# VectorE's side work moved between v and scan, experts' sums over two ticks, gate ranks by broadcast comparison, group norm sums on ScalarE

## The chip, the cores and the metric

The kernel runs on one core of a Trainium2 chip. The metric is device time in microseconds of one execution. Before the change it is 3911.06 us, the median of three runs (3910.29 to 3911.66). All data are fp32.

The names of the profile: PE is TensorE's matmul and PEld its weight load; DVE is VectorE, ACT is ScalarE, POOL is GpSimd, SP is SyncE, which here issues the DMAs.

## What is computed

Four images of 384 channels and 32 x 32 positions pass through two layers:

```python
# layer 0: group norm, then a selective scan in four directions over the image
x = x + _L0_conv_ref(_gn(x), ...)
#   dt = softplus(dts + bias); for each direction k and each position:
#     h = h * exp(dt * A) + (dt * u) * B        (16 states a channel)
#     y = sum over states of h * C
#   directions are summed, y + D * u, layer norm over channels, gelu
# layer 1: attention and a mixture of 4 experts, of which the best 2 count
t = _to_tokens(x)
t = t + _L1_attn_ref(_ln_t(t), Wq, Wk, Wv)      # causal, one head of 384
t = t + _L1_ffn_ref(_ln_t(t), gate_w, gate_b, w1, b1, w2, b2)
#   probs = softmax(scores); keep the top 2 of 4 and renormalise
#   out = sum over experts of masked * (gelu(x w1 + b1) w2 + b2)
```

## The kernel before

The program is laid out by hand in *ticks*. A tick is one unit of the scan: 32 channels by 4 states on the 128 partitions, 1024 positions along each. There are 4 images x 3 blocks of 128 channels x 4 directions x 4 groups of states x 4 groups of channels = 768 units, 192 an image. The loop over ticks writes instructions into the queues of the engines in a fixed order; nothing reorders them afterwards. In tick t it does this:

- `decay(t + 2)`: ScalarE computes exp(dt * A) (`da`, L505).
- `due`: functions that were put off to this tick. They stand ahead of v, that is after the scan of the tick before.
- `front(t)`: VectorE multiplies dt*u (`du4`, from SBUF) by B (`bc`, from SBUF) into `v` in PSUM (L512).
- `back(t - 1)`: GpSimd multiplies the states of the unit before by C (`h<-h,bc`, L525, "the product"). Both inputs are in SBUF. `order` makes it wait for v of tick t, so that it runs beside the scan.
- `inner`: functions put off to the place between v and scan; then `unpark` resumes the generators that had yielded "inner".
- `middle(t)`: VectorE's scan (L518), which reads `da` from SBUF and `v` from PSUM.
- `row`: after every fourth unit TensorE sums the states over partitions with the matrix `sel` (L550, the "y row").
- `fetch`: loads for coming units; then one step of `preparation` (group norm, projections and softplus of the next image), and `go_on`, which advances the side work and the work that waits in turn.

A generator that yields "wait", n is resumed n ticks later from the last place of the tick, so its VectorE work stands after the scan. One that yields "inner" is resumed in the next tick between v and scan.

The work behind the scan of an image is: `finish` (layer norm, gelu L702, residual add L707), `attention` (layer norm with L601, L633 and L649, queries, values, scores, softmax with L780 and L782, `normalise` with L794 and L795), `gates` (L881 to L923: softmax of four scores and their ranks, by loops over the four experts), and `experts` (matmuls L1027 and L1052, sums L1061 and L1064). `behind` runs attention and experts of one image after those of the other. They are metered: a tick may issue as much matmul as `pace`, in units of about a microsecond, PACE_A in attention and PACE_E in the experts. Image b's experts therefore run beside the scan of image b+1, and those of the last image alone.

Further names: `groupnorm` (statistics L302 and L303 on VectorE), `project_dt` (softplus L387, then du = dt * u, L395, stored by SP for the loads of later ticks), `evict` (L570). `slots` and `banks` are pools of SBUF buffers and PSUM banks that the program hands out in ticks. The buffer `a0` holds the attention's input `axn`, and then the experts' sums, which `store` writes out.

Of the kernel before, what the change touches and what calls it, by code (L numbers as in the profile page):

```python
# [15 lines left out]
P = 128  # L16
# [24 lines left out]
BANKS = 4  # L41
SLOTS = 8
PACE_A = 4.4
PACE_E = 3.3


@with_exitstack
def hybrid_kernel(
# [46 lines left out]
    clock = [-100]  # L95
    due = {}
    inner = {}

    def defer(ticks, f, where=due):
        where.setdefault(clock[0] + ticks, []).append(f)  # L100
# [99 lines left out]
    a4 = const.tile([P, K * NG, NQ], F32, tag="a4", name="a4")  # L200

    sel = const.tile([P, DJ], F32, tag="sel", name="sel")
    dump = const.tile([P, 1], F32, tag="dump", name="dump")
    nc.scalar.activation(a_raw, a_raw, AF.Exp)
    nc.scalar.activation(dump, eps, AF.Sqrt)
# [91 lines left out]
    def groupnorm(b, u):  # L297
        st = sm.tile([P, M, NH, 6], F32, tag="gn_st", name=f"gn_st_{b}")
        mv = sm.tile([P, M, 2], F32, tag="gn_mv", name=f"gn_mv_{b}")
        for m in range(M):  # L300
            for h in range(NH):
                nc.vector.bn_stats(st[:, m, h, :], u[m][:, h * 512 : (h + 1) * 512])  # L302
            nc.vector.bn_aggr(mv[:, m, :], st[:, m].rearrange("p h s -> p (h s)"))  # L303
            if b == 0 and m == 0:
                pgb = group_weights()
            yield "wait", 1
        if b == 0:
            nc.vector.tensor_scalar_mul(gback, pgb[:NGRP, :C], float(C // NGRP))
        mean_c = sm.tile([P, M], F32, tag="gn_mc", name=f"gn_mc_{b}")
        nc.vector.tensor_copy(mean_c, mv[:, :, 0])  # L310
        yield "wait", 1
        mean = sm.tile([P, M], F32, tag="gn_mean", name=f"gn_mean_{b}")
        ps = yield from over_group(mean_c, f"mean_{b}")
        nc.vector.tensor_copy(mean, ps)
        banks.give(f"gn_mean_{b}")
        dev = sm.tile([P, M], F32, tag="gn_dev", name=f"gn_dev_{b}")
        nc.vector.tensor_sub(dev, mean_c, mean)
        nc.vector.tensor_mul(dev, dev, dev)
        nc.vector.tensor_add(dev, dev, mv[:, :, 1])
        yield "wait", 1  # L320
        rstd = sm.tile([P, M], F32, tag="gn_rstd", name=f"gn_rstd_{b}")
        ps = yield from over_group(dev, f"var_{b}")
        nc.scalar.activation(rstd, ps, AF.Sqrt, bias=eps)
        banks.give(f"gn_var_{b}")
        yield "wait", 1
        nc.vector.reciprocal(rstd, rstd)
        nc.vector.scalar_tensor_tensor(mean, mean, -1.0, rstd, ALU.mult, ALU.mult)
        for m in range(M):
            if b == 0 and m == 1:
                nc.vector.tensor_scalar(  # L330
                    u[m], u[m], rstd[:, m : m + 1], mean[:, m : m + 1], ALU.mult, ALU.add
                )
            else:
                nc.scalar.activation(
                    u[m], u[m], AF.Identity, bias=mean[:, m : m + 1], scale=rstd[:, m : m + 1]
                )
            nc.sync.dma_start(xn_d[b][:, m, :], u[m])
            yield "wait", 1
# [26 lines left out]
    def project_dt(b, pair, m, u, xd):  # L365

        ks = PAIRS[pair]
        while not slots.ready(3 + pair):
            yield "wait", 1
        v = u[m]  # L370
        if pair == 1:
            v = slots.now(f"ut_{b}_{m}", P, L)
            nc.scalar.copy(v.rearrange("p (w h) -> p w h", h=HW), columns(u[m]))
        dts = [slots.now(f"dt_{b}_{k}_{m}", P, L) for k in ks]
        for h in range(NH):
            while not banks.ready(2):
                yield "wait", 1
            pss = [banks.now(f"pdt_{b}_{k}_{m}_{h}") for k in ks]
            for i, k in enumerate(ks):
                r = slice(64 * pair + 32 * i, 64 * pair + 32 * i + R)  # L380
                nc.tensor.matmul(  # L381
                    pss[i], wdt[r, m * P : (m + 1) * P], xd[r, bass.ts(h, 512)],
                    start=True, stop=True,
                )
            yield "wait", 1
            for i, k in enumerate(ks):
                nc.scalar.activation(  # L387
                    dts[i][:, bass.ts(h, 512)], pss[i], AF.Softplus, bias=dtb[:, k, m : m + 1]
                )
                banks.give(f"pdt_{b}_{k}_{m}_{h}")  # L390
        yield "wait", 1
        for i, k in enumerate(ks):
            nc.sync.dma_start(dts_d[b, k][0, m * P : (m + 1) * P, :], dts[i])
            du = yield from slots.take(f"du_{b}_{k}_{m}", P, L)
            nc.vector.tensor_mul(du, dts[i], v)  # L395
            yield "wait", 1
            nc.sync.dma_start(dts_d[b, k][1, m * P : (m + 1) * P, :], du)
            slots.give(f"dt_{b}_{k}_{m}", f"du_{b}_{k}_{m}")
        if pair == 1:
            slots.give(f"ut_{b}_{m}")  # L400
# [179 lines left out]
    def layernorm(dst, src, name, lag):  # L580
# [48 lines left out]
            rs, var[:, : n * P].rearrange("p (h t) -> p h t", t=P), AF.Sqrt, bias=eps  # L629
        )  # L630
        banks.give(f"var_{name}")
        yield "wait", 1
        nc.vector.reciprocal(rs, rs)  # L633
        yield "wait", lag
        backs = []
# [56 lines left out]
    def finish(b):  # L692

        yb = ybs[b]
        yield from layernorm(yb, yb, f"l0_{b}", 0)
        xrs = []
        for m in range(M):
            xr = yield from slots.take(f"xr_{b}_{m}", P, L)
            nc.sync.dma_start(xr, x[b, m * P : (m + 1) * P, :])
            xrs.append(xr)  # L700
        for m in range(M):
            nc.scalar.activation(  # L702
                yb[:, m, :], yb[:, m, :], AF.Gelu, bias=lnb[:, m : m + 1], scale=lnw[:, m : m + 1]
            )

            def add(m=m, xr=xrs[m]):
                nc.vector.tensor_add(yb[:, m, :], xr, yb[:, m, :])  # L707
                slots.give(f"xr_{b}_{m}")
                if m == M - 1:
                    finished.add(b)  # L710

            defer(1 + m // 2, add)

    def attention(b, yb, fx0):
        xn = ap0.tile([P, M, L], F32, tag="a0", name=f"axn_{b}")
# [61 lines left out]
        def softmax(i, ss, pr):  # L777
# [5 lines left out]
            for n, (o, e, ps) in enumerate(ss):  # L783
# [2 lines left out]
                    accum_out=nb[:, 2 + n : 3 + n],  # L786
                )
                banks.give(f"ss_{b}_{i}_{o}")
            defer(1, lambda: normalise(i, nb, len(ss)))

        def normalise(i, nb, n):
            wd = (i + 1) * P
# [75 lines left out]
    def gates(b, h, xn):  # L868
# [7 lines left out]
                    start=(c == 0), stop=(c == M - 1),  # L876
                )
        yield "pe", 5.0
        yield "wait", 1
        sc = sm.tile([P, 4, E], F32, tag="sc", name=f"sc_{name}")  # L880
        nc.vector.tensor_tensor(  # L881
            sc, pg[:, : 4 * E].rearrange("p (q e) -> p q e", e=E),
# [9 lines left out]
        nc.vector.tensor_reduce(red, sc, AX.X, ALU.max)  # L892
        nc.vector.tensor_tensor(sc, sc, over(red), ALU.subtract)
        nc.scalar.activation(sc, sc, AF.Exp)
        yield "wait", 1
        nc.vector.tensor_reduce(red, sc, AX.X, ALU.add)
        nc.vector.reciprocal(red, red)
        nc.vector.tensor_tensor(sc, sc, over(red), ALU.mult)
        cnt = sm.tile([P, 4, E], F32, tag="cnt", name=f"cnt_{name}")
        cmp = sm.tile([P, 4, E], F32, tag="cmp", name=f"cmp_{name}")  # L900
        nc.vector.memset(cnt, 0.0)
        for d in range(E):

            other = sc[:, :, d : d + 1]
            if d > 0:
                nc.vector.tensor_tensor(
                    cmp[:, :, :d], other.to_broadcast([P, 4, d]), sc[:, :, :d], ALU.is_gt
                )
                nc.vector.tensor_add(cnt[:, :, :d], cnt[:, :, :d], cmp[:, :, :d])
            if d < E - 1:  # L910
                nc.vector.tensor_tensor(
                    cmp[:, :, d + 1 :], other.to_broadcast([P, 4, E - 1 - d]),
                    sc[:, :, d + 1 :], ALU.is_ge,
                )
                nc.vector.tensor_add(cnt[:, :, d + 1 :], cnt[:, :, d + 1 :], cmp[:, :, d + 1 :])
            if d % 2:
                yield "wait", 1
        mk = sm.tile([P, 4, E], F32, tag="mk", name=f"mk_{name}")
        nc.vector.scalar_tensor_tensor(mk, cnt, 1.5, sc, ALU.is_lt, ALU.mult)
        nc.vector.tensor_reduce(red, mk, AX.X, ALU.add)  # L920
        nc.vector.tensor_scalar_add(red, red, 1e-9)
        nc.vector.reciprocal(red, red)
        nc.vector.tensor_tensor(mk, mk, over(red), ALU.mult)  # L923
        yield "wait", 1
        pm = yield from banks.take(f"pm_{name}")
        nc.tensor.transpose(pm[: 4 * E, :P], mk.rearrange("p q e -> p (q e)"), ident)
        yield "pe", 0.3
# [25 lines left out]
    def experts(b, acc, xns):  # L953
# [43 lines left out]
        def store(h):  # L997
            o = h * 512
            nc.sync.dma_start(out[b, :, o : o + 512].rearrange("(m p) l -> p m l", p=P), acc)
            if h + 1 < NH:  # L1000
                defer(4, lambda: load(h + 1))

        load(0)
        for h, e in [(h, e) for h in range(NH) for e in range(E)]:
# [37 lines left out]
            for c, (m, fh) in enumerate(TWO):  # L1042
# [15 lines left out]
                if fh == 1:  # L1058

                    def out_(m=m, ps=pss[m], e=e, tw=tw, fy=fy):  # L1060
                        nc.vector.scalar_tensor_tensor(  # L1061
                            ps, ps, b2s[:, e, m : m + 1], tw, ALU.add, ALU.mult
                        )
                        nc.vector.tensor_add(acc[:, m, :], acc[:, m, :], ps)  # L1064
                        banks.give(fy)

                    defer(2, out_, inner)
            if e == E - 1:
# [1 line left out]
                defer(4, lambda h=h: store(h))  # L1070

    pace = [PACE_E]

    def behind(b):
        while b not in finished:
            yield "wait", 1
        pace[0] = PACE_A
        fx0 = one.tile([P, M, 512], F32, tag="fx0", name=f"fx0_{b}")
# [79 lines left out]
    while t < NU + 4 or waiting or side or due or inner or parked:  # L1158
# [5 lines left out]
        done = None  # L1164
        if t < NU:
            done = front(t)
        if 1 <= t <= NU:
            back(t - 1, done)
        for f in inner.pop(t, []):
            f()  # L1170
        unpark()
        if t < NU:
            middle(t)
        if t >= 2 and t - 2 < NU and (t - 2) % NJ == NJ - 1:
# [62 lines left out]
```

## Time and profile before

| | us |
|---|---|
| median of the runs | 3911.06 |
| the profiled execution | 3911.65 |
| its span, first to last instruction | 3909.9 |
| busy PE | 3382.8 (87%) |
| busy DVE | 3096.5 (79%) |
| busy ACT | 1887.9 (48%) |
| busy POOL | 1809.5 (46%) |
| first v / last v | 49.3 / 3233.7 |

The mean granted TensorE clock is 0.899 of full speed.

The page cuts the span into 40 slices of 97.7 us; a digit is the busy share of a slice in tenths. A group line reads: line, engine, operation, output<-inputs, shapes, count | busy us in all, mean ns of one | idle time of the engine just before them, and what ended most of it. A line of the table by stretches reads: from:to in us, length, then busy us and number of records of PE, PEld, DVE, ACT and POOL, then granted clock, DMA share and GB/s. An fp32 matmul leaves two records. A timeline line reads: start, duration, engine, line, what it does, count, and in brackets the idle time before it and what ended that.

Some groups that the change concerns, as VectorE's groups by line have them:

```profile
L1061 DVE SCALAR_TENSOR_TENSOR fy<-fy,b2s,tw 128x512 f32<-128x512 f32 x96 | 72.3, 754 | 424.1 <-PE fy L1052 424.1
...
L302 DVE BATCH_NORM_STATS2 gn_st<-x 128x6 f32<-128x512 f32 x24 | 15.1, 673 | 3.6 <-DMA x<-in_x 3.6
L707 DVE TENSOR_TENSOR yb<-xr,yb 128x1024 f32<-128x1024 f32 x12 | 14.5, 1234 | 2.6 <-ACT yb L702 2.6
...
L782 DVE TENSOR_TENSOR nb<-nb 128x1 f32<-128x1 f32 x16 | 9.9, 619 | 0.5
```

### The profile page before, as it was taken

What the parts mean: (1) busy time and instruction counts of PE and PEld (TensorE: products, weight loads), DVE (VectorE), ACT (ScalarE), POOL (GpSimd) and SP (SyncE); (2) the same over time, 40 slices, a digit from 0 to 9 for tenths busy, and PEclk for the clock granted to TensorE, in tenths of its full rate; (3) what the DMA queues carried; (4) which work ended last, traced back from release to release, by engine and by line L of the source; (5) the groups of instructions that cost most, each with busy time, mean ns of one, the idle gap of its engine ahead of it and who ended that gap; (6) DMA issues with size and microseconds to landing.
All of it is one profiled execution on the core that took longest, in us unless ns stands there. A gap on an engine that the chain in (4) does not pass through costs nothing.

```text
span 3909.9 us, 32087 instructions
## 1 busy us (share of the span) xinstructions
PE 3382.8 (87%) x10623; PEld 1389.4 (36%) x10623; DVE 3096.5 (79%) x2258; ACT 1887.9 (48%) x1996; POOL 1809.5 (46%) x776
## 2 busy tenths in 40 slices
PE   4554655659899999978999999799999998999999
PEld 1100100015433334435433343354334334644444
DVE  6999999998999999979999899989999993110000
ACT  5442543446656656546656545555455453322121
POOL 2665666654555556535555566455566661000000
PEclk7665666679899999989999999899999999999999
DMA  5554545453576667535666666426566651132321
GB/s 192 203 183 148 197 147 188 162 189 127 191 239 208 236 223 241 184 112 190 223 211 214 212 218 213 162 105 227 179 214 213 222 187 44 61 90 82 96 82 55
DMA packets 406087, 671.85 MB, mean 172 GB/s; under 512 B 33265, under 2 KB 280353, under 8 KB 405921
## 3 DMA queue, kind: packets, MB, share of 16 engines
q1 hardware_dynamic: 399712, 669.41, 50.5%
q8 instruction: 84, 1.38, 0.1%
q10 hardware_dynamic: 6208, 0.39, 0.1%
q14 instruction: 83, 0.67, 0.1%
HBM read 597.75 MB, written 71.96 MB: 171 GB/s over the span
## 4 chain that ended last, share of the span: by engine, by line
DVE 49%; PE 38%; issue 5%; ACT 4%; DMA 2%; POOL 1%; DVEq 1%; SPq 0%; POOLq 0%; ACTq 0%
DVE h L518 29%; DVE v L512 15%; PE ph L1027 13%; PE fy L1052 12%; PE y L550 3%; PE ss L766 2%; PE pq L737 2%; PE pv L748 2%; PE po L832 1%; ACT da L505 1%; DVE fy L1061 1%; ACT ht L1016 1%; PE pxd L350 1%; DMA du<-dts 1%; DVE du L395 1%
## 5 line engine op out<-in xcount | busy, mean ns | idle before, releaser
L525 POOL TENSOR_TENSOR h<-h,bc 128x1024 f32<-128x1024 f32 x768 | 1808.4, 2355 | 1430.0 <-DVE v L512 1278.1
L518 DVE TENSOR_TENSOR_SCAN h<-da,v 128x1024 f32<-128x1024 f32 x768 | 1755.5, 2286 | 86.1 <-DVE v L512 1.5
L505 ACT ACTIVATE da<-dt,a 128x1024 f32<-128x1024 f32 x768 | 878.0, 1147 | 1232.3 <-DVE h L518 1171.7
L1027 PE MATMUL ph<-fx,w 128*128 128x512 f32 x2304 | 1027.5, 602 | 9.4 <-ACT ht L1012 3.8
L1052 PE MATMUL fy<-ht,w 128*128 128x512 f32 x2304 | 1015.8, 598 | 2.4 <-ACT dt L387 0.9
L512 DVE TENSOR_TENSOR v<-du,bc 128x1024 f32<-128x1024 f32 x768 | 947.2, 1233 | 38.5 <-DMA du<-dts 16.4
L550 PE MATMUL y<-h,sel 128*32 128x512 f32 x3072 | 703.7, 713 | 309.5 <-POOL h L525 295.3
L1027 PEld LDWEIGHTS ph<-fx,w 128*128 128x128 f32 x2304 | 434.8, 192 | 588.9 <-issue 530.7
L1052 PEld LDWEIGHTS fy<-ht,w 128*128 128x128 f32 x2304 | 435.5, 191 | 570.5 <-issue 551.7
L1012 ACT ACTIVATE ht<-ph,b1s 128x512 f32<-128x512 f32 x384 | 257.6, 679 | 453.0 <-PE ph L1027 452.5
L550 PEld LDWEIGHTS y<-h,sel 128*32 128x32 f32 x3072 | 118.3, 118 | 831.7 <-POOL h L525 579.2
L1061 DVE SCALAR_TENSOR_TENSOR fy<-fy,b2s,tw 128x512 f32<-128x512 f32 x96 | 72.3, 754 | 424.1 <-PE fy L1052 424.1
L1016 ACT ACTIVATE ht<-ht 128x3072 f32<-128x3072 f32 x64 | 176.9, 2764 | 0.8
L505 ACT ACT_TABLE_LOAD x110 | 141.1, 1283 | 14.4 <-DMA dt<-dts 12.5
L766 PE MATMUL ss<-axn,qt 128*128 128x512 f32 (+3 forms) x288 | 105.3, 512 | 7.4 <-ACT yb L844 5.8
L832 PE MATMUL po<-pt,vt 128*128 128x256 f32 x480 | 103.6, 363 | 6.7 <-ACT pt L728 6.7
L832 PEld LDWEIGHTS po<-pt,vt 128*128 128x128 f32 x480 | 91.9, 193 | 21.7 <-ACT pt L728 9.2
L780 DVE TENSOR_REDUCE nb<-ss 128x1 f32<-128x512 f32 (+3 forms) x48 | 26.2, 554 | 82.8 <-PE ss L771 64.6
L381 PE MATMUL pdt<-xd,wdt 12*128 12x512 f32 x184 | 61.5, 690 | 34.4 <-ACT xd L354 26.5
L766 PEld LDWEIGHTS ss<-axn,qt 128*128 128x128 f32 x288 | 52.3, 199 | 53.3 <-issue 36.5
L1064 DVE TENSOR_TENSOR fx<-fx,fy 128x512 f32<-128x512 f32 x96 | 65.9, 687 | 3.3
L1016 ACT ACT_TABLE_LOAD x50 | 64.2, 1283 | 0.9
(183 smaller groups left out, 1406.5 us busy)
## 6 DMA issues: line engine op xcount, KB each, us to landing
bc<-rows SPq DMA_DIRECT2D x384, 512.0 KB, 4.7
w<-in_w SPq DMA_DIRECT2D x384, 384.0 KB, 6.0
dt<-dts SPq DMA_DIRECT2D x192, 512.0 KB, 4.0
du<-dts SPq DMA_DIRECT2D x192, 512.0 KB, 6.1
dts<-dt SPq DMA_DIRECT2D x48, 512.0 KB, 4.9
dts<-du SPq DMA_DIRECT2D x48, 512.0 KB, 4.6
fx<-t2d SPq DMA_DIRECT2D x12, 768.0 KB, 6.0
tw<-mkd SPq DMA_DIRECT2D x32, 256.0 KB, 5.7
```

What stands on the lines that cost most here:

```text
L505: nc.scalar.activation(u["da"], spread["dt4", n], AF.Exp, scale=a4[:, g, u["q"] : u["q"] + 1])
L512: return nc.vector.tensor_tensor(u["v"], spread["du4", n], spread["bc", n][:, 0, :], ALU.mult)
L518: nc.vector.tensor_tensor_scan(u["h"][:, ::step], u["da"][:, ::step], u["v"][:, ::step], 0.0, op0=ALU.mult, op1=ALU.add,)
L525: product = nc.gpsimd.tensor_tensor(h, h, spread["bc", n][:, 1, :], ALU.mult)
L550: nc.tensor.matmul(y, sel, h, start=first, stop=last, tile_position=(0, jj * DJ))
L766: nc.tensor.matmul(ps[:, : e - o], qt[:, c, i * P : (i + 1) * P], xn[:, c, o:e], start=(c == 0), stop=(c == M - 1 and e <= i * P),)
L832: nc.tensor.matmul(pv[:, o:], vt[:, j, m * P : (m + 1) * P], pts[step][j // 4][:, j % 4, o:], start=False, stop=(j == nj - 1),)
L1012: nc.scalar.activation(ht[:, f, :], ps, AF.Identity, bias=bias)
L1016: nc.scalar.activation(ht, ht, AF.Gelu)
L1027: nc.tensor.matmul(ps, tiles[n][:, c, (f % 2) * P : (f % 2 + 1) * P], xns[h][:, c, :], start=(c == 0), stop=(c == M - 1),)
L1052: nc.tensor.matmul(pss[m], tiles[n][:, f, :], hts[fh][:, f, :], start=(fh == 0 and f == 0), stop=(fh == 1 and f == FH - 1),)
L1061: nc.vector.scalar_tensor_tensor(ps, ps, b2s[:, e, m : m + 1], tw, ALU.add, ALU.mult)
```

## The change

- Side work of VectorE that stood after the scan now stands between v and scan: du (L395), the residual add (L707), the reciprocals of the layer norms (L633), the softmax's normalise, and all of the gates.
- `back` is issued after `inner` and `unpark`. The product waits for the last of v, du and the residual add of its tick (the list `both`); other work between v and scan does not hold it back.
- The experts' two operations an output, the weighted bias and the sum, go into two successive ticks.
- The ranks of the gates are computed by two comparisons of all pairs, a mask `lower`, a maximum and a reduction, instead of loops over experts.
- For images 1 to 3 the group norm's sums come from ScalarE's accumulators (six passes over an image, three of Identity and three of Square) instead of VectorE's statistics.
- Attention of an image waits until the store of the image before has been issued (`stored`).
- PACE_E is 3.4 instead of 3.3.

```diff
-PACE_E = 3.3
+PACE_E = 3.4
...
+    both = []
...
+    lower = const.tile([P, E, E], F32, tag="lower", name="lower")
+    nc.vector.memset(lower, 0.0)
+    for e in range(1, E):
+        nc.vector.memset(lower[:, e, :e], 1.0)
...
-        for m in range(M):
+        mean_c = sm.tile([P, M], F32, tag="gn_mc", name=f"gn_mc_{b}")
+        if b > 0:
+            var_c = sm.tile([P, M], F32, tag="gn_vc", name=f"gn_vc_{b}")
+            sq = yield from slots.take(f"gn_sq_{b}", P, L)
+            for m in range(M):
+                nc.scalar.activation(
+                    sq, u[m], AF.Identity, scale=-1.0 / L, accum_out=mean_c[:, m : m + 1]
+                )
+                yield "wait", 1
+            for m in range(M):
+                nc.scalar.activation(
+                    sq, u[m], AF.Square, bias=mean_c[:, m : m + 1], accum_out=var_c[:, m : m + 1]
+                )
+                yield "wait", 1
+            slots.give(f"gn_sq_{b}")
+            yield "inner", 0
+            nc.vector.tensor_scalar_mul(mean_c, mean_c, -1.0)
+            nc.vector.tensor_scalar_mul(var_c, var_c, 1.0 / L)
+        for m in range(M) if b == 0 else ():
...
-        yield "wait", 1
         for i, k in enumerate(ks):
             nc.sync.dma_start(dts_d[b, k][0, m * P : (m + 1) * P, :], dts[i])
             du = yield from slots.take(f"du_{b}_{k}_{m}", P, L)
-            nc.vector.tensor_mul(du, dts[i], v)
+            yield "inner", 0
+            both[:] = [nc.vector.tensor_mul(du, dts[i], v)]
...
-        yield "wait", 1
+        yield "inner", 0
         nc.vector.reciprocal(rs, rs)
...
-                nc.vector.tensor_add(yb[:, m, :], xr, yb[:, m, :])
+                both[:] = [nc.vector.tensor_add(yb[:, m, :], xr, yb[:, m, :])]
...
-            defer(1 + m // 2, add)
+            defer(1 + m // 2, add, inner)
...
-            defer(1, lambda: normalise(i, nb, len(ss)))
+            defer(1, lambda: normalise(i, nb, len(ss)), inner)
...
         yield "pe", 5.0
-        yield "wait", 1
+        yield "inner", 0
...
         nc.scalar.activation(sc, sc, AF.Exp)
-        yield "wait", 1
+        yield "inner", 0
         nc.vector.tensor_reduce(red, sc, AX.X, ALU.add)
         nc.vector.reciprocal(red, red)
         nc.vector.tensor_tensor(sc, sc, over(red), ALU.mult)
+
+        cmp = [one.tile([P, 4, E, E], F32, tag=f"cmp{i}", name=f"cmp{i}_{name}") for i in range(2)]
+        each = sc.unsqueeze(3).to_broadcast([P, 4, E, E])
+        other = sc.unsqueeze(2).to_broadcast([P, 4, E, E])
+        nc.vector.tensor_tensor(cmp[0], other, each, ALU.is_gt)
+        nc.vector.tensor_tensor(cmp[1], other, each, ALU.is_ge)
+        yield "inner", 0
+        nc.vector.tensor_tensor(
+            cmp[1], cmp[1], lower.unsqueeze(1).to_broadcast([P, 4, E, E]), ALU.mult
+        )
+        nc.vector.tensor_tensor(cmp[0], cmp[0], cmp[1], ALU.max)
         cnt = sm.tile([P, 4, E], F32, tag="cnt", name=f"cnt_{name}")
-        nc.vector.memset(cnt, 0.0)
-        for d in range(E):
...
+        nc.vector.tensor_reduce(cnt, cmp[0], AX.X, ALU.add)
+        yield "inner", 0
...
+            else:
+                stored.add(b)
...
-                        nc.vector.tensor_add(acc[:, m, :], acc[:, m, :], ps)
-                        banks.give(fy)
+
+                        def add():
+                            nc.vector.tensor_add(acc[:, m, :], acc[:, m, :], ps)
+                            banks.give(fy)
+
+                        defer(1, add, inner)
...
-        while b not in finished:
+        while b not in finished or (b > 0 and b - 1 not in stored):
             yield "wait", 1
...
-        if 1 <= t <= NU:
-            back(t - 1, done)
+        both[:] = [done]
         for f in inner.pop(t, []):
             f()
         unpark()
+        if 1 <= t <= NU:
+            back(t - 1, both[0])
```

More of the change, by code (lines that the diff above doesn't have):

```diff
@@ L308, in groupnorm @@
             nc.vector.tensor_scalar_mul(gback, pgb[:NGRP, :C], float(C // NGRP))
-        mean_c = sm.tile([P, M], F32, tag="gn_mc", name=f"gn_mc_{b}")
-        nc.vector.tensor_copy(mean_c, mv[:, :, 0])
+            var_c = mv[:, :, 1]
+            nc.vector.tensor_copy(mean_c, mv[:, :, 0])
         yield "wait", 1
@@ L318, in groupnorm @@
         nc.vector.tensor_mul(dev, dev, dev)
-        nc.vector.tensor_add(dev, dev, mv[:, :, 1])
+        nc.vector.tensor_add(dev, dev, var_c)
         yield "wait", 1
@@ L898, in gates @@
         nc.vector.tensor_tensor(sc, sc, over(red), ALU.mult)
-        cnt = sm.tile([P, 4, E], F32, tag="cnt", name=f"cnt_{name}")
-        cmp = sm.tile([P, 4, E], F32, tag="cmp", name=f"cmp_{name}")
-        nc.vector.memset(cnt, 0.0)
-        for d in range(E):
[L904 to L917, printed above, removed]
+        cmp = [one.tile([P, 4, E, E], F32, tag=f"cmp{i}", name=f"cmp{i}_{name}") for i in range(2)]
[8 more added lines that the diff above has]
+        nc.vector.tensor_tensor(cmp[0], cmp[0], cmp[1], ALU.max)
+        cnt = sm.tile([P, 4, E], F32, tag="cnt", name=f"cnt_{name}")
+        nc.vector.tensor_reduce(cnt, cmp[0], AX.X, ALU.add)
+        yield "inner", 0
         mk = sm.tile([P, 4, E], F32, tag="mk", name=f"mk_{name}")
@@ L923, in gates @@
         nc.vector.tensor_tensor(mk, mk, over(red), ALU.mult)
-        yield "wait", 1
+        yield "wait", 2
         pm = yield from banks.take(f"pm_{name}")
@@ L1072, in hybrid_kernel @@
     pace = [PACE_E]
+    stored = set()
     def behind(b):
-        while b not in finished:
+        while b not in finished or (b > 0 and b - 1 not in stored):
             yield "wait", 1
```

## The prediction

> **What bounds the kernel now.** I read the page's 40 slices first, then the chain of waits, then the busy time by stretches, then the groups by line, the VectorE waits, and last the timeline of single ticks.
>
> ```profile
> PE   4554655659899999978999999799999998999999
> ...
> DVE  6999999998999999979999899989999993110000
> ...
> DVE 49%; PE 38%; issue 5%; ACT 4%; DMA 2%; POOL 1%; DVEq 1%; SPq 0%; POOLq 0%; ACTq 0%
> ```
>
> VectorE is full until slice 33 (the last scan), then TensorE alone works. The table by stretches (length, then busy PE, PEld, DVE) tells more:
>
> ```profile
> 430.00:810.00 380.00, 223.33 (x471) 35.42 (x469) 364.12 (x213) 168.84 (x154) 232.32 (x99) 0.63 0.48 170
> ...
> 1030.00:1600.00 570.00, 555.92 (x1723) 224.61 (x1725) 539.87 (x400) 337.84 (x328) 325.55 (x138) 0.98 0.64 217
> 1600.00:1760.00 160.00, 134.43 (x518) 60.68 (x509) 135.23 (x88) 80.23 (x92) 73.02 (x31) 0.91 0.41 142
> ...
> 1865.00:2450.00 585.00, 571.11 (x1741) 229.22 (x1743) 547.02 (x385) 337.19 (x326) 333.88 (x142) 0.98 0.63 214
> ...
> 2690.00:3235.00 545.00, 538.01 (x1668) 217.60 (x1667) 524.02 (x349) 295.95 (x283) 326.85 (x139) 1.00 0.61 202
> ```
>
> While image 0 is scanned (the first line) VectorE alone is the bound. In the three expert stretches (lines 2, 4, 5; 138, 142 and 139 ticks by POOL's count) VectorE and TensorE are both full: TensorE lacks only 14.1+13.9+7.0 = 35.0 us. This decides what a saving on VectorE is worth there.
>
> A tick is one v (L512) and one scan (L518), with POOL's product (L525) of the tick before beside the scan:
>
> ```profile
> L525 POOL TENSOR_TENSOR h<-h,bc 128x1024 f32<-128x1024 f32 x768 | 1808.4, 2355 | 1430.0 <-DVE v L512 1278.1
> L518 DVE TENSOR_TENSOR_SCAN h<-da,v 128x1024 f32<-128x1024 f32 x768 | 1755.5, 2286 | 86.1 <-DVE v L512 1.5
> ...
> L512 DVE TENSOR_TENSOR v<-du,bc 128x1024 f32<-128x1024 f32 x768 | 947.2, 1233 | 38.5 <-DMA du<-dts 16.4
> ```
>
> On the timeline, 548 of 767 ticks hold nothing else and take 3.69 us from v to v (1.233 + 0.13 until the scan starts + 2.287 + 0.035). With work between v and the scan (63 ticks with L1061 and L1064: 4.85 us), the tick less that work is 3.41 us; with a single long operation there (L570, L649) 3.375; with work after the scan (37 ticks with L395: 4.77 us) 3.49. Work between v and scan thus hides up to 0.31 us, work after the scan 0.20. POOL's product starts 0.17 us after v ends.
>
> One place shows the danger:
>
> ```profile
> 955.67 1.25 DVE L512 TENSOR_TENSOR v<-du,bc 128x1024 f32<-128x1024 f32 x1
> 956.84 1.14 DVE L780 TENSOR_REDUCE nb<-ss 128x1 f32<-128x512 f32 x2
> 958.01 1.44 DVE L782 TENSOR_TENSOR nb<-nb 128x1 f32<-128x1 f32 x1
> 959.37 2.27 DVE L518 TENSOR_TENSOR_SCAN h<-da,v 128x1024 f32<-128x1024 f32 x1
> ...
> 957.09 2.35 POOL L525 TENSOR_TENSOR h<-h,bc 128x1024 f32<-128x1024 f32 x1 [1.26 <-DVE v L512]
> ```
>
> A one-element tensor_tensor, 0.16 us elsewhere, takes 1.44 us and ends 15 ns after the product (959.44). L780, with one PSUM input, is not held.
>
> [...] Here bursts of expert matmuls run at 0.435 us a record with experts alone waiting for nothing, so I take the 97% as nearly full, but leave a rival for it.
>
> **Part by part**, against the profiled execution (3911.65 us, span 3909.9; 0.6 above the median of 3911.06).
>
> *Group norm sums* (images 1 to 3): 18 L302 and 9 L303 leave. Nine ticks of 4.976 become 3.69: 9 x 1.29 = 11.6 us; two new 3-element operations an image cost 0 to 2.2 [...], 0.3 taken. Three of the ticks lie in image 0's scan (all real, -3.5), three in the next attention (-3 taken), three in an expert stretch (0). ScalarE gains 18 passes of 1.23 (as L334) and 0.195 for each accumulator read (as L784's), 26 us; it is at 48%, and a decay is issued two ticks before its scan. With that cover gone they would cost up to 26.
>
> *Experts' sums in two ticks*: L1061 and L1064 stood in 69 ticks, now in about 123. 54 more ticks with work after v, 54 x 0.31 = 17 us of VectorE. But a unit of the pace is a us of TensorE (2.6 are charged for three matmuls, six records of 0.435), so PACE_E 3.4 gives it 0.10 us more in each of 419 ticks, 42 us, and there are 35 us of room. VectorE's saving is thus not paid out there: if TensorE's gaps fall to 10 us, these stretches grow by 42 - 25 = 17 us (bounds: -10, if the gaps aren't real limits, and +30, with today's gaps kept). Next late there: TensorE. In return each image's experts need 4.4 ticks less (8 x (12 x 2.6 + 6 x 5.1) = 494 units, by 3.3 and by 3.4), so the next image's finish and attention, into which they run over today, have less matmul in the way: up to 2 x 4.4 x 3.3 = 29 us for two images, at least 0; -12 taken, some 40%, since these ticks are VectorE's in part.
>
> *du and the residual add*: 46 du and 9 adds go between v and scan, the product waiting for them (nothing is queued behind it on POOL but the next product). Product end then falls 0.29 us after the next v begins; v bears 0.12, so 0.165 is lost: 3.52 + du against 3.49 + du, 1.5 us in all. The first du of each pair is asked for one scan (2.4 us) earlier after its softplus. Of the 25 us that du waits today, most lies in ticks where TensorE is behind; 0 to +18, inside the +17 above. Each du's store follows on SP at most a tick later, ahead of its use by most of an image: 0.
>
> *Waiting for the store*: `stored` holds attention until the previous image's sums are written. VectorE's waits name it:
>
> ```profile
> DVE axn L601 <- DMA out<-fx: 11.8, 2, 9.4
> ```
>
> (This is between 1030 and 3235 us: total, times, longest.) 11.8 goes, between 0 and 15; 11 taken, since the wait is now in ticks with other work.
>
> *Gates*: 24 compare and add instructions and a memset, some 2.1 us a gate, become 5 of about 1.1. But all of it now stands between v and scan, four ticks a gate, and only du and the add hold the product back. In each tick an operation with two SBUF inputs comes later than 0.17 us after v (in the changed kernel's lines: subtract L917, normalise L922, max L933, last L942) and is blocked until the product ends, 3.76 after the start of v; the scan behind it waits too. Ticks of 4.05, 5.01, 4.475 and 4.53 become about 6.05, 6.45, 6.35 and 6.05: +6.8 a gate. If L933 is early enough, +4.6. Six of eight gates lie in the scan (the others meet no POOL): 28 to 41 us. Three stand at the end of attention, where it counts (3 x 6.8, 12 taken as some ticks share the block with other work); three in expert stretches where TensorE's backlog covers them (0; uncovered 20).
>
> *The rest*: reciprocals -1, the softmax's normalise +1; four memsets at the start lie under the wait for the first image.
>
> *Tail*: in the built order, 24 matmuls of image 2's last expert stand behind the last y row today, 12 in the changed kernel, all ahead of the layer norm. That starts at about the same time, but isn't interrupted, as it is now:
>
> ```profile
> 3265.65 5.42 PE L1052 MATMUL fy<-ht,w 128*128 128x512 f32 x12
> ...
> 3271.79 5.32 PE L1052 MATMUL fy<-ht,w 128*128 128x512 f32 x12
> ...
> 3278.04 1.75 DVE L649 TENSOR_TENSOR yb<-yb,rb_l 128x1536 f32<-128x1536 f32 x1 [4.29 <-PE rb_l L639]
> ```
>
> Reciprocal at about 3266.2 instead of 3268.0, both broadcasts at once, product at 3270.9 instead of 3279.8: 8.9; and the store's 2.5 in front of L601: -11 (-8 to -17). From the first query matmul on, TensorE is full either way.
>
> Sum: -3.5 - 3 + 17 - 12 + 1.5 - 11 + 12 - 11 = **-10**: 3911.65 - 10, say **3901 us**.
>
> **Rivals.** (1) [...] All six gates are on the path: 41 instead of 12, 3930. For it: L782 blocks without exception where it overlaps the product. Against: the expert stretches wait for TensorE anyway. It decides once over 22 of the 41 us are not covered. (2) *TensorE has more room than its busy time says*: the expert stretches give -10 instead of +17, 3874. For it: between 2677 and 3235 VectorE had no wait over 0.25 us, so the stretch is VectorE's. Against: 98.7% busy. (3) *Nothing*: what VectorE saves in the scan TensorE takes back, and the tail's gain pays the locks, 3911.
>
> **Numbers.** Forecast 0.45 (own range 3889 to 3914; 0.33 of it faster), rival 1 0.30, rival 2 0.20, rival 3 0.05. A change of 0.2%, 7.8 us, is what can be told from none. Faster 0.33 + 0.20 = 0.53, same 0.12 + 0.05 = 0.17, slower 0.30. Range 3870 to 3935.
>
> **What would show it.** Right: L917, L922 and L942 near 2 us each in the scan; TensorE over 98% in the expert stretches and these no shorter for the same number of ticks; no wait of L601 for the store; nothing of image 2 between the last layer norm's matmuls. Wrong: short gate operations beside a product; expert ticks clearly below 4.0 us; or new long waits of du for softplus, which would push it above 3930.

## The result and the profile after

The changed kernel takes 3957.99 us (median of four runs, 3949.73 to 3958.9), the kernel before 3910.68 in the same comparison: ratio 1.0117 (after over before), 95% interval 1.0099 to 1.0134. It is 47 us slower where 10 us of gain were forecast. The profiled execution took 3958.9 us, its span is 3957.1.

The chain of waits of the changed kernel, by engine (shares of the span):

```profile
PE 55%; DVE 32%; issue 5%; ACT 4%; DMA 2%; POOL 1%; SPq 1%; DVEq 0%; POOLq 0%; ACTq 0%
```

Before it was DVE 49% and PE 38%: the end now hangs on TensorE for longer. Where the 47 us lie shows when the ticks are summed on the timeline, from the start of one v to the start of the next:

| ticks | what runs beside the scan | before, us | after, us | difference |
|---|---|---|---|---|
| until the first v | | 49.3 | 47.4 | -1.9 |
| 0 to 191 | nothing (image 0's scan) | 739.8 | 736.5 | -3.3 |
| 192 to 239 | finish and attention of image 0 | 227.4 | 221.4 | -6.0 |
| 240 to 383 | experts of image 0, projections of image 2 | 594.5 | 657.8 | **+63.3** |
| 384 to 439 | finish and attention of image 1 | 276.6 | 272.0 | -4.6 |
| 440 to 575 | experts of image 1, projections of image 3 | 557.8 | 555.5 | -2.3 |
| 576 to 629 | finish and attention of image 2 | 251.1 | 253.5 | +2.4 |
| 630 to 766 | experts of image 2 | 537.3 | 540.6 | +3.3 |
| tail, from the last v on | image 3 alone | 676.1 | 672.4 | -3.8 |

One stretch of 144 ticks lost 63 us; all the rest together won 16. The waits of the changed kernel between 1005 and 1663 us, which is that stretch (us in total, times, longest):

```profile
DVE du L419 <- ACT dt L411: 55.8, 6, 11.5
POOL h L549 <- DVE du L419: 46.8, 7, 14.9
```

Six times VectorE stood still ahead of a du until ScalarE had done its softplus (dt), and GpSimd's product, which waits for du, stood with it. The groups of the changed kernel on VectorE (the number behind the bar's second stroke is idle time before the group):

```profile
L419 DVE TENSOR_TENSOR du<-dt,ut 128x1024 f32<-128x1024 f32 x24 | 29.3, 1220 | 38.2 <-ACT dt L411 38.2
L419 DVE TENSOR_TENSOR du<-dt,x 128x1024 f32<-128x1024 f32 x22 | 26.8, 1220 | 34.9 <-ACT dt L411 34.9
...
L917 DVE TENSOR_TENSOR sc<-sc,red 128x16 f32<-128x16 f32 x8 | 9.7, 1214 | 0.3
L940 DVE TENSOR_SCALAR red<-red 128x4 f32<-128x4 f32 x8 | 9.6, 1198 | 0.3
L922 DVE TENSOR_TENSOR sc<-sc,red 128x16 f32<-128x16 f32 x8 | 8.5, 1064 | 0.3
...
L933 DVE TENSOR_TENSOR cmp<-cmp,cmp 128x64 f32<-128x64 f32 x8 | 1.8, 225 | 0.3
```

du waited 25 us before the change, 73 now. The kernel before:

```profile
L395 DVE TENSOR_TENSOR du<-dt,ut 128x1024 f32<-128x1024 f32 x24 | 30.1, 1252 | 23.0 <-PE ph L1027 16.5 <-ACT da L505 5.7 <-PE fy L1052 0.8
L395 DVE TENSOR_TENSOR du<-dt,x 128x1024 f32<-128x1024 f32 x22 | 27.9, 1267 | 2.0 <-ACT dt L387 2.0
```

L917, L922 and L940 show the hold by GpSimd's product that was feared: 1.1 to 1.2 us on average where 0.17 is the unhindered time. Each was held four times of eight, mostly for 2.2 us, and ended 24 to 32 ns after the product then. The max L933 is never held.

du is made in pairs, for two directions of the scan at a time, and an image has six pairs. The six waits are those of the first du of each pair of image 2. One of them, on the changed kernel's timeline:

```profile
1243.34 1.27 ACT L411 ACTIVATE dt<-pdt,dtb 128x512 f32<-128x512 f32 x2
1243.61 1.23 DVE L536 TENSOR_TENSOR v<-du,bc 128x1024 f32<-128x1024 f32 x1
1244.09 12.79 PE L1048 MATMUL ph<-fx,w 128*128 128x512 f32 x24
...
1249.19 0.69 ACT L1033 ACTIVATE ht<-ph,b1s 128x512 f32<-128x512 f32 x1 [2.12 <-PE ph L1048]
1251.76 0.69 ACT L1033 ACTIVATE ht<-ph,b1s 128x512 f32<-128x512 f32 x1 [1.89 <-PE ph L1048]
1252.47 1.28 ACT L411 ACT_TABLE_LOAD   x1
1253.77 1.27 ACT L411 ACTIVATE dt<-pdt,dtb 128x512 f32<-128x512 f32 x2
1254.48 1.22 DVE L419 TENSOR_TENSOR du<-dt,x 128x1024 f32<-128x1024 f32 x1 [9.64 <-ACT dt L411]
...
1255.63 2.28 DVE L542 TENSOR_TENSOR_SCAN h<-da,v 128x1024 f32<-128x1024 f32 x1
1255.85 2.36 POOL L549 TENSOR_TENSOR h<-h,bc 128x1024 f32<-128x1024 f32 x1 [12.18 <-DVE du L419]
```

Read it from below. du waits for the softplus of the second half. That stands on ScalarE's queue behind two moves of ht (L1033), though its own input pdt was written by 1244.15 (L405), 8.3 us before its table load begins; and those moves wait for an expert's first matmuls (ph), on which TensorE works for 12.8 us without a break. VectorE needs nothing of the expert here, but it waits for that queue, as du stands in the middle of its tick. In all six cases one or two moves of ht stand ahead of a softplus. In the first four a move waits for TensorE; in the last two (ticks 323 and 341) it does not, and the expert's gelu (L1037, 2.76 us after a table load of 1.28) stands ahead of it.

### The profile page after: what moved, and what is told of

Same layout as the page of the kernel before. It is cut to its first block, busy times and chain, and to the rows that moved or that the text cites. A ratio compares the mean times of both kernels' runs of the same rounds, so it can differ in the third digit from the quotient of the medians.

```text
span 3957.1 us, 32028 instructions
## 1 busy us (share of the span) xinstructions
PE 3420.5 (86%) x10623; PEld 1391.2 (35%) x10623; DVE 3100.7 (78%) x2174; ACT 1906.4 (48%) x2028; POOL 1810.1 (46%) x776
## 4 chain that ended last, share of the span: by engine, by line
PE 55%; DVE 32%; issue 5%; ACT 4%; DMA 2%; POOL 1%; SPq 1%; DVEq 0%; POOLq 0%; ACTq 0%
PE ph L1048 21%; DVE h L542 20%; PE fy L1073 20%; DVE v L536 10%; PE y L574 5%; PE pq L761 2%; PE ss L790 2%; PE pv L772 2%; PE po L856 1%; DMA w<-in_w 1%; ACT da L529 1%; POOL h L549 1%; DMA du<-dts 1%; PE pxd L374 1%; PE pdt L405 1%
## 5 line engine op out<-in xcount | busy, mean ns | idle before, releaser
L574 PE MATMUL y<-h,sel 128*32 128x512 f32 x3072 | 712.2, 721 | 325.8 <-POOL h L549 311.2
L1033 ACT ACTIVATE ht<-ph,b1s 128x512 f32<-128x512 f32 x384 | 260.0, 682 | 600.5 <-PE ph L1048 600.3
L1037 ACT ACTIVATE ht<-ht 128x3072 f32<-128x3072 f32 x64 | 176.9, 2764 | 0.8
L529 ACT ACT_TABLE_LOAD x106 | 136.0, 1283 | 13.6 <-DMA dt<-dts 11.7
L405 PE MATMUL pdt<-xd,wdt 12*128 12x512 f32 x184 | 76.5, 793 | 47.8 <-ACT xd L378 25.9
```

What stands on the lines that cost most here:

```text
L405: nc.tensor.matmul(pss[i], wdt[r, m * P : (m + 1) * P], xd[r, bass.ts(h, 512)], start=True, stop=True,)
L529: nc.scalar.activation(u["da"], spread["dt4", n], AF.Exp, scale=a4[:, g, u["q"] : u["q"] + 1])
L574: nc.tensor.matmul(y, sel, h, start=first, stop=last, tile_position=(0, jj * DJ))
L1033: nc.scalar.activation(ht[:, f, :], ps, AF.Identity, bias=bias)
L1037: nc.scalar.activation(ht, ht, AF.Gelu)
```

## The experiments

Three theories at first: A, du is asked for too soon after softplus; B, gate operations held until GpSimd's product ends (the lock, in the expectations), as L782 was before for up to 1.71 us; C, PACE_E 3.4 is too much for TensorE. All runs were compared with the kernel before on the same chip.

**The tick between softplus and du put back.**

```diff
+        yield "wait", 1
         for i, k in enumerate(ks):
```

> The changed kernel with the tick between softplus and du put back (yield wait 1 ahead of the loop over du); du stays between v and scan. Theory A (du is asked for too early: in the changed kernel VectorE sits idle 73 us before du, 25 before the change, 56 of it in image 0's expert stretch): du's idle time falls to under 25 us and the time to 3900 to 3915. Theory B [...]: 3950 or more, since the gates are as they were. Theory C (PACE_E 3.4 is too much for TensorE): 3945 or more.

3912.60 us, ratio 1.0007 (0.9998 to 1.0015): 45 us came back, du's idle time fell to 28 us, ticks 240 to 383 to 607.1 us. As theory A had it, but this edit also makes a pair of du come every 19 ticks and not every 18, which matters below.

**PACE_E back at 3.3.**

> The changed kernel with PACE_E 3.3. Theory C: TensorE's backlog goes, du waits 25 us as before, 3900 to 3915. Theory A: the backlog of a burst of matmuls is still there, since du still follows softplus by one tick: 3935 to 3965. Theory B: 3950 to 3965.

3937.32 us, 1.0072 (1.0057 to 1.0088): far from theory C, near the lower end of what theory A expected, and 21 us of the 47 came back. An expert is now 18.7 ticks long. The six waits are 5.1, 5.9, 8.6, 8.0, 3.2 and 1.4 us: they change from pair to pair, which theory A alone does not explain.

**The product behind the gates.** In four places of `gates`:

```diff
-        nc.vector.tensor_tensor(mk, mk, over(red), ALU.mult)
+        both[:] = [nc.vector.tensor_tensor(mk, mk, over(red), ALU.mult)]
```

> The changed kernel with the product held back behind the last gate operation of each tick (both is set there too), so that no gate operation can meet it. Theory B: L917, L922 and L940 fall from 1.1 to 1.2 us to about 0.17, and 20 to 40 us come back: 3918 to 3938. Theory A: at most 10 us, 3945 to 3958, since VectorE waits in image 0's expert stretch for TensorE anyway.

3942.47 us, 1.0084 (1.0069 to 1.0099), 15.5 us less than the changed kernel. Its groups:

```profile
L917 DVE TENSOR_TENSOR sc<-sc,red 128x16 f32<-128x16 f32 x8 | 1.4, 175 | 0.3
...
L940 DVE TENSOR_SCALAR red<-red 128x4 f32<-128x4 f32 x8 | 1.4, 170 | 0.3
```

The hold is real, and holding the product back brings 15 us, between what the two theories expected. The du waits stay (69.5 us).

**11 ticks instead of 12 between two projections.**

```diff
-                yield "wait", 0 if b == 0 and m == 0 else 12
+                yield "wait", 0 if b == 0 and m == 0 else 11
```

> The changed kernel with 11 instead of 12 ticks between two projections, so that a pair of du comes every 17 ticks (as before the change) and not every 18, close to an expert's 18.2. Theory A with a resonance (every du of image 2 meets the same place of an expert, a burst of first matmuls): the waits of du in image 0's expert stretch spread out, some vanish, total idle before du 30 to 50 us, time 3925 to 3945. Theory A without it: 3950 to 3962. Theories B and C: 3950 to 3962.

3922.89 us, 1.0032 (1.002 to 1.0045), a little below what the resonance was to give. du's idle time 46 us, the six waits 3.2 to 9.3 us. A tick between projections is worth 35 us without any change between softplus and du: the first hint that the place in the expert decides.

**du's part of the change alone,** on the kernel before.

```diff
-        yield "wait", 1
         for i, k in enumerate(ks):
...
-            nc.vector.tensor_mul(du, dts[i], v)
+            yield "inner", 0
+            both[:] = [nc.vector.tensor_mul(du, dts[i], v)]
```

> The kernel before with the du part of the change alone: no tick between softplus and du, du between v and scan, the product behind it; gates, group norm, experts and pace as before. Theory A (du is asked for too early): slower than before by itself; VectorE's idle time before du rises from 25 us to 40 to 70, time 3922 to 3950. If du costs only together with PACE_E 3.4 and the rest: under 3918.

3896.86 us, 0.9965 (0.9952 to 0.9978): *faster* than before by 13 us, with 18 us of idle before du. Theory A in its plain form falls. At 3.3 an expert has 18.7 ticks, and the first pair stands in tick 243 and not 251; four of image 2's six pairs met no wait at all.

**du exactly as before the change,** in the changed kernel.

> The changed kernel with du exactly as before the change: one tick after softplus, behind the scan instead of ahead of it, the product not held by it; that is some 2.4 us later than in the changed kernel and 1.3 us earlier than with the tick put back. Theory A, by the time between softplus and du: about 2.4 us less for each of the 10 long waits, du's idle 45 to 55 us, time 3930 to 3943. If instead the place between v and scan is what costs (scan and product waiting with it): 3905 to 3915, as good as with the tick put back.

3926.65 us, 1.0041 (1.0026 to 1.0055), du's idle 42.8 us. Less than theory A expected by both measures, but not as good as with the tick put back, and it too makes the pairs come every 17 ticks. Its pairs stand in the same ticks as those of the run with 11 ticks (240, 257, ... 325). There du is asked for 2.4 us sooner, and the whole takes 3922.89. So the time between softplus and du decides nothing between these two, nor does the place: that scan and product wait together with du costs nothing that shows here.

**Both repairs,** the tick and the gates:

> The changed kernel with both repairs: the tick between softplus and du put back, and the product held behind the gates. Theory A [...]: the two add up, 3912.6 - 15 = 3892 to 3902, faster than before. If the lock is hidden once du no longer waits: 3907 to 3914.

3899.16 us, 0.9973 (0.9963 to 0.9983). They add up (15.5 less than 3912.6 would be 3897).

**Both repairs with PACE_E 3.3:**

> Both repairs and PACE_E 3.3. If 3.4 is right for the repaired kernel, this is 5 to 12 us slower than it (the last image's tail takes the matmuls): 3900 to 3912. If TensorE is still too full at 3.4: equal or up to 8 us faster, 3886 to 3898.

3896.31 us, 0.9962 (0.9947 to 0.9977), 3 less than with 3.4, intervals overlapping. du waits only 8 us in this run, but the tail is 698 us long and not 671. All six of image 2's pairs stand at record 55 to 57 of an expert's 72 second matmul records.

**The phase.** For each first du of a pair I counted which of the expert's records TensorE was at when v of that tick ended. An image's experts run as eight passes, four experts for each half of the positions; a pass, called an expert here, has 72 records of first matmuls (ph) and 72 of second ones (fy). In the changed kernel the six stand at record 65, 49, 49, 48, 53 and 52 of the first 72. A pair of du now comes every 18 ticks (two halves, twice two for du, 12 of waiting; before 2 + 1 + 2 + 12 = 17), and an expert at pace 3.4 takes 494 / 8 / 3.4 = 18.2 (494 units an image, as in the prediction). Theory P: whoever meets the end of the first matmuls once, meets it six times. Two runs were to test it by starting the projections of image 2 at another tick (33 in the first, 42 in the second):

```diff
-        while clock[0] < IMAGE * (b - 1) + 24:
+        while clock[0] < IMAGE * (b - 1) + (33 if b == 2 else 24):
```

> The changed kernel with the projections of image 2 begun 9 ticks later (24 becomes 33), nothing else; softplus and du stay as close as they are. Theory P (the phase: a pair of du comes every 18 ticks and an expert takes some 18.2, so that in image 0's expert stretch six softplus in a row stand on ScalarE behind moves of ht that wait for the expert's first matmuls, at record 48 to 65 of 72): half an expert later they meet the second matmuls, where no ht move is due. The six waits of 6 to 11 us fall under 1 us each, du's idle from 73 to 20 to 35 us, ticks 240 to 384 take 600 to 615 us and not 658, time 3903 to 3918. Theory A (one tick between softplus and du is too short at any place): waits stay at 6 to 11, time 3945 to 3960.

> The control: the projections of image 2 begun 18 ticks later, about a whole expert. Theory P: the same place in the expert again, five or six waits of 6 to 11 us, 3940 to 3960. If the time of the start matters and not the phase (less to do at once at the start of the stretch): like the run with 9 ticks, under 3920.

3955.32 (1.0115, 1.01 to 1.013) and 3957.66 us (1.0119, 1.0104 to 1.0134), but both say nothing of the phase: image 2's group norm, which stands ahead of its projections, ends only in tick 238, and the two starts are ticks 225 and 234, so every du of image 2 stayed in its tick. They serve as repeats of the changed kernel. The same holds for image 2 in the next two; the second also moves image 3's pairs (its start is 37), and that does happen:

> The product behind the gates and image 2's projections 9 ticks later. [...] the run with 9 ticks less 15 us, 3888 to 3902.

> The same, and image 3's projections 13 ticks later, so that its pairs too meet second matmuls. Theory P: the 14 us that du waits in image 1's expert stretch go as well, 5 to 14 us less than the run before it, 3876 to 3895.

3937.88 (1.007, 1.0053 to 1.0087) and 3946.57 us (1.0093, 1.0078 to 1.0108). As image 2 did not move, the first shows the gates' repair once more: 17.4 us less than 3955.32. In the second, four of image 3's six pairs came to record 24 of the second matmuls, where the gelu of the expert stands on ScalarE: waits of 2.5 to 4.6 us there, 6.6 us at the first pair, and no gain. A wrong guess of where the queue is short.

**The pairs really moved.**

```diff
         yield from groupnorm(b, u)
+        yield "wait", 9 if b == 2 else 0
```

> The changed kernel with a wait of 9 ticks behind image 2's group norm, which moves all its du from ticks 251 ... 344 to 259 ... 351; nothing else. (The two runs before that changed the start of the projections left these ticks where they were, since the projections of the image before end later than that start.) Theory P (phase): from record 48 to 65 of an expert's first 72 the pairs move to the middle of its second 72, where ScalarE has no ht move; the six waits of 6 to 11 us fall under 2 us each, ticks 240 to 384 take 600 to 620 us and not 658, time 3903 to 3922. Theory A (one tick between softplus and du is too short wherever it falls): waits of 6 to 11 us, 3945 to 3960.

3908.22 us, 0.9992 (0.9983 to 1.0001): of the 47 us all are gone. Ticks 240 to 383 take 611.1 us, the other stretches stay within 1.7 us of the changed kernel's. The same pair of this run:

```profile
1250.24 1.23 DVE L537 TENSOR_TENSOR v<-du,bc 128x1024 f32<-128x1024 f32 x1
...
1252.31 1.26 ACT L411 ACTIVATE dt<-pdt,dtb 128x512 f32<-128x512 f32 x2 [2.39 <-PE pdt L405]
...
1253.03 1.23 DVE L419 TENSOR_TENSOR du<-dt,x 128x1024 f32<-128x1024 f32 x1 [0.97 <-ACT dt L411]
1253.05 3.27 PE L1074 MATMUL fy<-ht,w 128*128 128x512 f32 x7 [0.77 <-ACT dt L411]
```

TensorE is at the second matmuls (fy), no ht move stands ahead of softplus, and du waits 0.97 us and not 9.64. The first du of the six pairs wait 0, 2.7, 1.0, 4.3, 0 and 1.6 us, at record 38 to 48 of the second 72; two of them stay above the 2 us that were expected.

**The control, a whole expert later:**

```diff
+        yield "wait", 18 if b == 2 else 0
```

> The control: a wait of 18 ticks in the same place, du of image 2 in ticks 268 ... 362, about a whole expert (18.2 ticks) later. Theory P: the same place in the expert again, at least four waits of 6 to 11 us, 3938 to 3960. If it is only that the projections leave the start of the expert stretch: under 3922, as with 8 ticks.

3945.63 us, 1.0088 (1.0073 to 1.0103), waits of 12.5, 7.1, 7.9, 3.2, 8.0 and 7.1 us at record 42 to 60 of the first matmuls. The second of them:

```profile
1232.66 2.76 ACT L1038 ACTIVATE ht<-ht 128x3072 f32<-128x3072 f32 x1
...
1235.33 0.67 ACT L1034 ACTIVATE ht<-ph,b1s 128x512 f32<-128x512 f32 x1
1236.01 1.28 ACT L411 ACT_TABLE_LOAD   x1
...
1237.31 1.27 ACT L411 ACTIVATE dt<-pdt,dtb 128x512 f32<-128x512 f32 x2
...
1238.03 1.23 DVE L419 TENSOR_TENSOR du<-dt,ut 128x1024 f32<-128x1024 f32 x1 [7.12 <-ACT dt L411]
```

Eight ticks later helps, 17 do not: it is the phase. This is shown. That the phase acts through ScalarE's queue, by moves of ht and gelu ahead of softplus, is read from the timelines; no run changed that queue alone.

**Gates free and the pairs moved:**

> The product behind the gates, and image 2's du 8 ticks later. [...] 12 to 20 us less than the run with 8 ticks alone, 3886 to 3906, and faster than before.

3892.86 us, 0.9959 (0.9944 to 0.9974), the lowest median of all, if not told apart from the 3896 of two runs above; 15.4 less than without the gates' repair. It beats both kernels, the one before by 18 us.

## Why the prediction was wrong

The step that failed is the term for du, "the first du of each pair is asked for one scan (2.4 us) earlier", priced "0 to +18, inside the +17". It was not inside: du's idle time rose by 48 us and ticks 240 to 383 by 63. The mechanism was named, waits of du for softplus where TensorE is behind, and the text gave "new long waits of du for softplus" as what would push the time above 3930. The size was taken from the waits of the kernel before, whose pairs, 17 ticks apart, drift through an expert of 18.7 ticks (in image 0's expert stretch they meet record 53, 48, 32, 18 and 6 of the first 72). Both numbers that lock them were in hand: the code of `project_dt` gives 18 ticks, and the 4.4 ticks that an image's experts save give 18.2 an expert. I never set them side by side. The run with the pairs moved puts 50 us (3957.99 against 3908.22) on it.

Rival 1, slower by the holds of the gates, had the sign but not the main cause: freeing the gates brings back 15 us of the 47. That the time came out on its side is luck. Nor was L782 held without exception: of the nine that met the product before, seven ended 14 to 18 ns after it (taking up to 1.71 us), but two that met only its last 0.11 and 0.04 us took 0.16 us like the others.

The other steps:

- *Group norm*: -3.5 in image 0's scan, measured -3.3 there with the rest of what changed in it.
- *Gates*: 12 us on the path of 28 to 41; freeing them brings 15.5, 13.4, 17.4 and 15.4 us in the four pairs of runs that differ in this alone. The size is near, but by luck, for the place was wrong. The 12 were put into attention, and nothing into the expert stretches, where TensorE's backlog was to cover them. With the gates free the three attention stretches together change by -2.5 us (in the changed kernel) and +2.6 (with the pairs moved), the three expert stretches by -17.2 and -13.4; the expert stretch of image 2, with one gate in it, gives 5.5 to 6.2 us in all four. L917 and L922 were held as foretold, 2.2 to 2.3 us (L922 once 1.1), where they met the product; L933 was not. In the fourth tick not L942 but L940 was held, a tensor_scalar of four elements with one input; it ended 24 to 26 ns after the product, so L942 behind it was free (175 ns). That two inputs in SBUF decide which operations are held was my assumption. L940, with one, was held for 2.2 us; the reduction L935, with one too, ran beside the product in six ticks and took 219 to 221 ns. What sets the two apart, no run shows.
- *The new 64-element operations*: 218 to 225 ns each, so that a gate's five take the 1.1 us that were estimated.
- *Store*: VectorE's 11.8 us ahead of the attention's L601 are gone; the two stretches with finish and attention of images 1 and 2 together won 2.2 us, though, not the 23 that the store and the *fill* (the 4.4 ticks that an image's experts save, -12) were to bring there. The fill is not seen in either pair of runs that differ in PACE_E alone: from 3.3 to 3.4 these two stretches grow by 4.2 us in the changed kernel and by 3.3 with both repairs, while the tail shrinks by 11.7 and 27.5. So what the pace gives, it gives in the tail. Some of the gates' holds stand in these stretches too; what else took the store's gain was not tried.
- *Expert stretches +17*: with the pairs moved, the three stretches of experts take 611.1, 555.3 and 540.9 us against 594.5, 557.8 and 537.3, +17.7. But the gates, priced at nothing here, are 13.4 of it: with them free as well, 608.7, 550.5 and 534.7, +4.3 (in a profiled execution 9 us above its run's median). So the agreement with +17 is luck. What is left lies between the forecast and rival 2's -10 and decides neither. TensorE is busy for 98.2, 98.8 and 99.6% of these stretches then; in the changed kernel it was 95.0, 97.9 and 98.8%.
- *Tail -11*: -3.8. The uninterrupted layer norm was right: from its first matmul to the first query matmul 41.5 us (3309.5 to 3351.0), before 48.7. But it starts 24.7 us after the start of the last v and not 20.1, where "at about the same time" was forecast. All 24 records of the last 12 matmuls stand ahead of it, as foretold:

```profile
3299.07 10.57 PE L1073 MATMUL fy<-ht,w 128*128 128x512 f32 x24
...
3309.47 5.31 PE L617 MATMUL mu_l<-yb,mean_w 128*128 128x512 f32 x12
```

Open stays whether a tick more between softplus and du helps at the same place in the expert: every run that gave it also moved the pairs. And the 13 us that du's part alone gains lie in image 1's expert stretch (543.1 us against 557.8), where the kernel before waited 9.9 and 5.4 us for du and this run never over 0.5; that this is phase again is likely, but was not tested.

## What to carry to other kernels

Where two periodic pieces of work share one engine's queue, as du's softplus and the experts' moves share ScalarE's here, set their periods side by side before and after a change: 17 against 18.7 ticks drifts, 18 against 18.2 locks, and a wait that used to come once (5.2 us ahead of one du in image 0's expert stretch, at most 1.4 ahead of the others) then comes every time (six of 6.3 to 11.5 us). A lock is not bad in itself: in the run with both repairs and PACE_E 3.3, 19 against 18.7 ticks, all six pairs stand within three records of each other, among the second matmuls, and the longest of their waits is 1.2 us. Price a wait for another engine's queue at the worst phase that the new periods allow, and not as the mean of today's waits. In this kernel, moving one image's du by eight ticks was worth 50 us, more than any saving of work that was counted for the change.

## What was unexpected of the hardware

A tensor_scalar over four fp32 elements with one SBUF input (L940) was held by GpSimd's product as long as operations with two inputs: 2.2 us in each of the four cases where the product ran, ending 24 to 26 ns after it, 0.17 us in the other four and with the product held behind the gates. A max over 64 elements with two inputs (L933), second behind v, got through each time (225 ns). It starts 0.16 us after v ends and the product 0.17 us after, so it came first by some 10 ns.
